# A four-way gated scan whose output is summed by accumulating transposes, with the layer norm on turned tiles and a new order of the parts

## The chip, the core and the metric

The kernel runs on one core of one Trainium2 chip. A core has a tensor engine (PE, with a separate row PEld for its weight loads), a vector engine (DVE), a scalar engine (ACT), a general engine (POOL, GpSimd) and a queue that issues transfers (SP). Each engine takes its instructions in the order of the program and waits for the others by semaphores. The metric is the time of one execution on the device in microseconds; the median of three runs before the change is 16998.98 us (16979.7 to 17001.8).

## The reference

The model has two layers. The second, a bidirectional selective scan, is the same in both kernels and matters here only because it starts after the first is done. The first layer, cut to what it computes, for x of shape (8, 192, 64, 64):

```python
x = conv1x1(x, W_in)                       # 192 -> 384 channels
x = depthwise_conv3x3(x, W_dw) + b_dw
x_proxy = conv1x1(x, W_xd)                 # 384 -> 16 channels
ws, Ls, Us, Ds = (conv1x1(x_proxy, w) for w in (W_w, W_l, W_u, W_d))
xs = [x, x.T, x reversed, x.T reversed]    # 4 directions over the last axis
Gl, Gm, Gr = normalize_w(ws)               # each / (|Gl| + |Gm| + |Gr| + 1e-7)
# scan in chunks of 8 columns; step over the column in the chunk, all chunks at once
h = 0
for each column j of a chunk:
    h = L * x + Gl * h_up + Gm * h + Gr * h_down    # neighbours along the rows
out = h * Us + xs * Ds
y = sum over the 4 directions of w_m[d] * out[d]
y = layernorm2d(y)                         # over the 384 channels
y = grn(y)                                 # scaled by each channel's norm over the image
return conv1x1(y, W_out)                   # 384 -> 192 channels
```

All of it is float32.

## The kernel before

The 384 channels are three blocks of 128 partitions. An image has 64 x 64 positions, handled as rows of 512 elements.

Each of the 8 images passes through two stages. The first, of 24 *units* (three channel blocks by eight strips of 8 rows), makes the convolved input `xc`. A unit's `begin` (from L137) multiplies by `W_in` on PE (L143), writes the centre tap from ACT (L147) and the two side taps by ACT (L159) and POOL (L162); its `unit` (L188) adds the six other taps on DVE (L196). The last units are followed by `proxy` (L173), which makes the 16-channel proxy `xp`, four times over on four groups of 32 partitions, so that gate products of different groups stand in different rows of the PE array.

The second stage is the *scan*: 3 channel blocks x 8 columns j x 4 directions d = 96 steps per image. A `Step` consists of small parts: `gates` (L240: four products of 16 rows by 512 columns, for the decay lambda and the three gates), `decay` (L252, ACT copies lambda out of PSUM), `entry` (L256, POOL, lambda times input), `magnitude` (L245, ACT, absolute values), `norm` (L275, two DVE additions), `log` and `exp` (L280, L285, ACT: a first reciprocal), `newton` (L290, two DVE operations that refine it), `neighbour` 0, 1, 2 (L259, DVE: gate times shifted state), `pair` (L265, POOL), `total` (L269, PE: two products with the identity add up the neighbours in the bank q), `mix` (L297, DVE), `state` (L301, POOL), `up` (L305, PE: the products for D, `pd`, and U, `pu`), `direct` (L308, ACT copies pd to dx), `bypass` (L312, POOL: dx times input, and at the fourth direction the third's dx is added to it, the joined bypass), `output` (L317, DVE: hu = pu times state), `add` (L321, PE: products with the identity that accumulate hu and dx of four directions in the bank yp) and `store` (L337, ACT copies yp to y once in four steps). Steps with j = 0 have no previous state, and do without the gates, the norm, the total and the mix.

PSUM has eight banks: one each tagged gl, gm, q and yp, and two each tagged gr and c. Lambda's product, pd and pu take turns on the two banks of c.

`scan` (L347) writes out the order by hand. One round of its loop (L361 to L385) works on four steps at once: the newest (`s0`), the two before, the oldest (`s3`, whose adds are made) and the next, whose gates are made. `tc.manual_schedule()` keeps each engine's instructions in the order in which the program gives them. On PE a round is total of s1, gates of the next, add hu of s3, add dx of s3, then D and U of s1. On DVE it is neighbours 2 and 0 of s0, Newton of s1, neighbour 1, the two additions of norm, hu of s2 and the mix of s1. So hu of s2 stands ahead of the mix of s1.

`Norm` (L388) does the layer norm of the image before, in ten parts beside the first units of the next image; units are left out after two of the parts. Channels are on partitions, so the mean over channels and the mean of squares are products with a constant matrix on PE (L399, L413), with three DVE subtractions (L404), three ACT squares (L408), a log, an exponent (L419, L420) and three DVE operations for the root (L421 to L423), three POOL products (L442) and three ACT squares with a sum (L430) for each j. `project_out` (L460) follows: the channel scaling, folded into the output weights, and 16 output products (L499), copies (L503) and transfers to `mid`, spread over the later units by the list `PARTS`.

Of the kernel before, what the change touches and what calls it, by code (L numbers as in the profile page):

```python
# [15 lines left out]
P = 128  # L16
CM = 192
KM = 96
# [15 lines left out]
JOINED = 2  # L34
UNITS = NC * CHUNK

PARTS = [0] * 8 + [1, 1, 1, 2, 1, 1, 1, 1, 1, 1, 1, 1, 1, 1, 1, 1]
# [4 lines left out]
ROWS = {GL: (0, 0), GM: (1, 0), GR: (2, 0), GLAM: (3, 0), GU: (0, 1), GD: (1, 1)}  # L42


@with_exitstack
def kernel(ctx: ExitStack, tc: tile.TileContext, x, w_in, dw, vecs, w_xd, w_gate, w_m, w_out, mid):
# [9 lines left out]
    big = ctx.enter_context(tc.tile_pool(name="l0_big", bufs=6))  # L56
# [46 lines left out]

    states = []
# [8 lines left out]
    class Image:  # L113
# [6 lines left out]
        def __init__(self, b):  # L120
            self.b = b
            self.x = x[b].rearrange("(k p) h w -> p k (h w)", p=KM)
            self.xc, self.xins, self.banks = [], {}, {}
            self.xp = p1.tile([P, CHUNK, CHUNK, HW], F32, tag="xp", name=f"xp_{b}")
            self.u = 0
            for u in range(4):
                self.load(u)
            for u in range(2):
                self.begin(u)
# [7 lines left out]
        def begin(self, u):  # L137
            c, r = divmod(u, CHUNK)
            if r == 0:
                self.xc.append(big.tile([P, HW, HW], F32, tag="big", name=f"xc_{self.b}_{c}"))  # L140
# [5 lines left out]
            self.load(u + 4)  # L146
# [26 lines left out]
        def proxy(self, r):  # L173
            pp = bank("c", f"pp_{self.b}_{r}")
            for c in range(NC):
                nc.tensor.matmul(
                    pp,
                    w_xd_sb[:, c, :],
                    self.xc[c][:, 8 * r : 8 * r + 8, :].rearrange("p h w -> p (h w)"),
                    start=(c == 0),  # L180
                    stop=(c == NC - 1),
                )
            nc.scalar.copy(
                self.xp[:, :, :, 8 * r : 8 * r + 8].rearrange("p j n h -> p h n j"),
                pp.rearrange("p (h n j) -> p h n j", n=CHUNK, j=CHUNK),
            )

        def unit(self):  # L188

            u, self.u = self.u, self.u + 1  # L190
            if u + 2 < UNITS:
                self.begin(u + 2)
            c = u // CHUNK
            for t in (0, 1, 2, 6, 7, 8):
                acc, part = self.shifted(u, t)
                nc.vector.scalar_tensor_tensor(  # L196
                    acc, part(self.banks[u]), dw_sb[:, c, t : t + 1], acc, ALU.mult, ALU.add
                )
            if u >= UNITS - CHUNK + 2:
                self.proxy(u % CHUNK - 2)  # L200
# [17 lines left out]
    class Step:  # L218
# [4 lines left out]
        def __init__(self, tag, xc, xp, wg, d, j):  # L223
            self.tag, self.xc, self.xp, self.wg, self.d, self.j = tag, xc, xp, wg, d, j
# [7 lines left out]
        def gate(self, kind, tag):  # L232
# [4 lines left out]
            nc.tensor.matmul(dst, self.wg[r, at, self.d, :], flat(self.xp[r, self.j]), start=True, stop=True)  # L237
# [37 lines left out]
        def norm(self):  # L275
            if self.j:
                for i in range(2):
                    nc.vector.tensor_add(self.g[2], self.g[2], flat(self.ab[i]))  # L278
# [11 lines left out]
        def newton(self):  # L290

            if self.j:
                s, rc = self.g[2], flat(self.rc)
                nc.vector.scalar_tensor_tensor(s, s, 1e-7, rc, ALU.add, ALU.mult)
                nc.vector.scalar_tensor_tensor(rc, s, 2.0, rc, ALU.subtract, ALU.mult)
# [16 lines left out]
        def bypass(self):  # L312
            nc.gpsimd.tensor_mul(self.dx, self.dx, direction(self.xc, self.d, self.j))  # L313
            if self.d == JOINED + 1:
                nc.gpsimd.tensor_add(self.dx, self.dx, self.before.dx)
# [5 lines left out]
        def add(self, i):  # L321


            if self.d == 0 and i == 0:
                self.yp = bank("yp", f"yp_{self.tag}")
            elif i == 0:
                self.yp = self.before.yp
            if i == 0 or self.d != JOINED:
                nc.tensor.matmul(
                    self.yp,  # L330
                    ident,
                    flat((self.hu, self.dx)[i]),
                    start=(self.d == 0 and i == 0),
                    stop=(self.d == ND - 1 and i == 1),
# [6 lines left out]
    class Nothing:  # L341


        def __getattr__(self, part):
            return lambda *args: None

    def scan(b, xc, xp):  # L347


        ys, steps = [], [Nothing()] * 4  # L350
        for c in range(NC):
            wg = w_gate_sb[:, :, :, c * P : (c + 1) * P]
            ys.append(big.tile([P, CHUNK, CHUNK * HW], F32, tag="big", name=f"y_{b}_{c}"))
            for j in range(CHUNK):
                steps += [Step(f"{b}_{c}_{j}_{d}", xc[c], xp, wg, d, j) for d in range(ND)]
                for step in steps[-ND:]:
                    step.y = ys[c][:, j, :]
        for before, step in zip(steps[4:], steps[5:]):
            step.before = before
        steps += [Nothing()] * 4  # L360
        for s3, s2, s1, s0, ahead in zip(steps, steps[1:], steps[2:], steps[3:], steps[4:]):  # L361
            s2.state()
            s0.neighbour(2)
            s0.neighbour(0)
            s0.entry()
            s1.newton()
            s1.total()
            s0.neighbour(1)
            s0.pair()
            s0.magnitude(2)  # L370
            s2.direct()
            ahead.gates()
            s0.norm()
            s0.log()
            ahead.decay()
            s2.bypass()
            s3.add(0)
            s2.output()
            s3.add(1)
            ahead.magnitude(0)  # L380
            s1.up()
            s0.exp()
            s1.mix()
            ahead.magnitude(1)
            s3.store()  # L385
        return ys

    class Norm:  # L388


        def __init__(self, b, ys):
            self.b, self.ys = b, ys
            self.ss = p1.tile([P, NC, CHUNK], F32, tag="ss", name=f"ss_{b}")
            self.pm, self.squares, self.var, self.rstd = {}, {}, {}, {}

        def mean(self, j):
            self.pm[j] = bank("gr", f"pm_{self.b}_{j}")
            for c in range(NC):
                nc.tensor.matmul(self.pm[j], mean_w, self.ys[c][:, j, :], start=(c == 0), stop=(c == NC - 1))  # L399

        def center(self, j):
            for c in range(NC):
                y = self.ys[c][:, j, :]
                nc.vector.tensor_sub(y, y, self.pm[j])  # L404
                sq = self.squares[j, c] = p2.tile(
                    [P, T], F32, tag=("ab0", "ab1", "dx")[c], name=f"sq_{self.b}_{j}_{c}"
                )
                nc.scalar.activation(sq, y, AF.Square)  # L408

        def variance(self, j):  # L410
            self.var[j] = bank("c", f"pv_{self.b}_{j}")
            for c in range(NC):
                nc.tensor.matmul(self.var[j], mean_w, self.squares[j, c], start=(c == 0), stop=(c == NC - 1))  # L413

        def root(self, j):

            r = self.rstd[j] = p2.tile([P, T], F32, tag="rc", bufs=3, name=f"rstd_{self.b}_{j}")
            v = self.var[j]
            nc.scalar.activation(r, v, AF.Ln, bias=eps5)  # L419
            nc.scalar.activation(r, r, AF.Exp, scale=-0.5)  # L420
            nc.vector.scalar_tensor_tensor(v, v, 1e-5, r, ALU.add, ALU.mult)  # L421
            nc.vector.tensor_mul(v, v, r)
            nc.vector.scalar_tensor_tensor(r, v, 3.0, r, ALU.subtract, ALU.mult)  # L423

        def response(self, j):

            for c in range(NC):
                y = self.ys[c][:, j, :]
                sq = p2.tile([P, T], F32, tag="hu", name=f"sq2_{self.b}_{j}_{c}")
                nc.scalar.activation(  # L430
                    sq,
                    y,
# [6 lines left out]
        def scale(self, j):  # L439
            for c in range(NC):  # L440
                y = self.ys[c][:, j, :]
                nc.gpsimd.tensor_mul(y, y, self.rstd[j])  # L442

        def parts(self):

            for j in range(CHUNK + 2):
                if j < CHUNK:
                    self.mean(j)
                if 0 <= j - 1 < CHUNK:
                    self.root(j - 1)  # L450
                    self.scale(j - 1)
                if j > 1:
                    self.response(j - 2)
                if j < CHUNK:
                    self.center(j)
                yield
                if j < CHUNK:
                    self.variance(j)

    def project_out(b, ys, ss):  # L460

        gr = p1.tile([P, NC + 1], F32, tag="gr", name=f"gr_{b}")
        gx, rg = gr[:, :NC], gr[:, NC:]
        nc.vector.tensor_reduce(gx, ss, AX.X, ALU.add)
        nc.scalar.activation(gx, gx, AF.Sqrt)
        nc.scalar.preload_act_table_set(ACT_SET)
        yield
        pg = bank("c", f"pg_{b}", (P, 1))
        for c in range(NC):
            nc.tensor.matmul(pg, mean_w, gx[:, c : c + 1], start=(c == 0), stop=(c == NC - 1))  # L470
        nc.vector.tensor_scalar_add(rg, pg, 1e-6)
        nc.vector.reciprocal(rg, rg)
# [615 lines left out]
```

## Time and profile before

| what | value |
| --- | --- |
| median of 3 runs | 16998.98 us (16979.7 to 17001.8) |
| the profiled execution | 16973.27 us |
| its span on the core | 16971.4 us |
| mean granted clock of TensorE | 0.903 of full |
| busy share of the span: PE, DVE, ACT, POOL | 84%, 90%, 72%, 89% |
| first layer, until its last projection is done | about 5973 us of the span |
| scan steps in the first layer | 768, of which 672 with j > 0 |

The page gives each engine's busy time and, in forty equal slices, its busy share in tenths; the row PEclk is the clock that TensorE was granted, in tenths of full speed. In groups and timeline rows, "q<-q,ident 128x512 f32 x4" is the output, the inputs, the shape and the number of instructions; a float32 product of 512 columns is two instructions. Matmuls overlap, so the start of the next block, and not a block's own length, tells what a block costs. The bracket behind a row of waits names the instruction that ended an idle time.

### The profile page before, as it was taken

Reading aid. Unit: us, or ns where it says so; the run is one execution under the profiler, and the core shown is the slowest. Engines: PE = TensorE matmul, PEld = TensorE weight load, DVE = VectorE, ACT = ScalarE, POOL = GpSimd, SP = SyncE. Lnnn points to the kernel's source line nnn. Section 1 sums busy time; section 2 is a strip of 40 time slices with the busy share of each in tenths; the row PEclk is TensorE's granted clock in tenths of the full one; section 3 lists DMA queues with packets and bytes.
Section 4 is the critical chain, followed back from the end, with each engine's and each line's share of the span. In section 5 each row is a group of like instructions: output and inputs, shape, how many; then the busy total and the mean of one; then the engine's idle time right before and its main releaser. Section 6 shows DMA issues by size and latency. Waiting matters only on the chain.

```text
span 16971.4 us, 183983 instructions
## 1 busy us (share of the span) xinstructions
PE 14236.2 (84%) x58320; PEld 7740.8 (46%) x58320; DVE 15279.7 (90%) x14474; ACT 12149.0 (72%) x25963; POOL 15186.0 (89%) x9955
## 2 busy tenths in 40 slices
PE   9999999999999977777777777777777777777777
PEld 2333333333333345555555555555555555555555
DVE  8888888888887779999999999999999999999999
ACT  5656666666666667777777777777777777777777
POOL 7787978778787779999999999999999999999999
PEclk8999999999999988888888888888888888888888
DMA  1001010010100022222222222222222222222222
GB/s 30 24 7 30 1 30 8 23 30 1 30 1 26 2 96 105 105 105 105 104 106 104 106 104 106 104 106 104 106 104 106 104 106 104 106 104 106 104 103 87
DMA packets 695519, 1249.43 MB, mean 74 GB/s; under 512 B 311768, under 2 KB 378672, under 8 KB 694544
## 3 DMA queue, kind: packets, MB, share of 16 engines
q1 hardware_dynamic: 694144, 1237.37, 19.9%
q8 instruction: 461, 7.55, 0.2%
q14 instruction: 514, 4.21, 0.1%
q10 hardware_dynamic: 400, 0.29, 0.0%
HBM read 1178.77 MB, written 58.72 MB: 73 GB/s over the span
## 4 chain that ended last, share of the span: by engine, by line
POOL 23%; DVE 15%; DMA 9%; ACT 8%; issue 6%; PE 4%; SPq 0%; DVEq 0%; POOLq 0%; ACTq 0%
POOL hs L861 15%; DVE da L875 11%; DMA c_sb<-bc 8%; ACT da L867 3%; POOL hs L882 3%; DVE hs L882 3%; POOL lg L768 1%; POOL e L766 1%; POOL dt L770 1%; PE pz L712 1%; POOL dtx L773 1%; DMA b_sb<-bc 1%; PE pc L700 1%; PE dbl_ps L731 1%; PE yp L887 1%
## 5 line engine op out<-in xcount | busy, mean ns | idle before, releaser
L861 POOL TENSOR_TENSOR hs<-dtx,b_sb 128x1022 f32<-128x1022 f32 x3072 | 7157.5, 2357 | 61.3 <-DMA b_sb<-bc 35.2
L875 DVE TENSOR_TENSOR_SCAN da<-da,hs 128x1024 f32<-128x1024 f32 x2560 | 5852.3, 2286 | 421.6 <-ACT hs L870 391.2
L867 ACT ACTIVATE da<-dt,a 128x512 f32<-128x512 f32 x6144 | 4247.9, 691 | 182.6
L887 PEld LDWEIGHTS yp<-ident,hs 128*128 128x128 f32 x24576 | 3022.9, 150 | 1000.1 <-issue 743.0
L887 PE MATMUL yp<-ident,hs 128*128 128x128 f32 x24576 | 3353.4, 287 | 67.1 <-DVE hs L882 59.8
L882 DVE TENSOR_TENSOR hs<-da,c_sb 128x1024 f32<-128x1024 f32 x2560 | 3129.2, 1222 | 88.7
L237 PE MATMUL g<-xp,w_gate_sb 16*128 16x512 f32 x8640 | 1812.6, 657 | 60.5 <-ACT dx L310 51.6
L700 PE MATMUL pc<-xr,conv_diag 128*128 128x512 f32 x3072 | 1542.8, 627 | 182.8 <-ACT dt L756 162.5
L878 ACT COPY state<-da 128x2 f32<-128x2 f32 x2560 | 400.8, 157 | 1626.0 <-DVE hs L882 1617.1
L820 PE MATMUL po<-out_w,z 128*128 128x192 f32 x3072 | 828.3, 420 | 748.2 <-ACT xc L704 365.3
L263 DVE TENSOR_TENSOR q<-g,h 128x512 f32<-128x512 f32 x2016 | 1353.7, 685 | 113.2 <-PE g L237 68.6
L273 PE MATMUL q<-q,ident 128*128 128x512 f32 x2688 | 1333.1, 618 | 0.0
L875 DVE TENSOR_TENSOR_SCAN hs<-da,hs 128x1024 f32<-128x1024 f32 x512 | 1168.8, 2283 | 143.1 <-ACT hs L870 87.4
L283 ACT ACTIVATE rc<-g,eps 128x512 f32<-128x512 f32 x672 | 462.2, 688 | 1119.2 <-DVE g L278 1119.2
L678 PE MATMUL pi<-xT,in_w 96*128 96x512 f32 x1536 | 955.2, 760 | 317.3 <-ACT z L812 312.2
L313 POOL TENSOR_TENSOR dx<-dx,xc 128x512 f32<-128x512 f32 x768 | 1079.7, 1406 | 155.2 <-ACT dx L310 132.7
L882 POOL TENSOR_TENSOR hs<-hs,c_sb 128x1024 f32<-128x1024 f32 x512 | 1206.7, 2357 | 1.8 <-ACT state L878 1.6
L712 PE MATMUL pz<-in_w,xT 96*128 96x384 f32 x2048 | 849.6, 541 | 421.3 <-ACT y L843 231.9
L237 PEld LDWEIGHTS g<-xp,w_gate_sb 16*128 16x128 f32 x8640 | 493.5, 188 | 1304.9 <-DVE q L263 395.9
L820 PEld LDWEIGHTS po<-out_w,z 128*128 128x128 f32 x3072 | 653.0, 245 | 829.6 <-ACT xc L704 395.3
L267 POOL TENSOR_TENSOR q<-q,q 128x512 f32<-128x512 f32 x672 | 853.6, 1270 | 193.7 <-DVE q L263 188.1
L257 POOL TENSOR_TENSOR lam<-lam,xc 128x512 f32<-128x512 f32 x672 | 942.1, 1402 | 32.1 <-ACT lam L254 32.1
(145 smaller groups left out, 25264.4 us busy)
## 6 DMA issues: line engine op xcount, KB each, us to landing
b_sb<-bc SPq DMA_DIRECT2D x1024, 512.0 KB, 9.1
c_sb<-bc SPq DMA_DIRECT2D x1024, 512.0 KB, 8.9
xin<-in_x_dram SPq DMA_DIRECT2D x192, 384.0 KB, 3.6
mid<-ot SPq DMA_DIRECT2D x128, 192.0 KB, 2.1
xt<-mid SPq DMA_DIRECT2D x64, 384.0 KB, 10.0
out_dram<-y SPq DMA_DIRECT2D x64, 384.0 KB, 2.6
bc<-dbl SPq DMA_DIRECT2D x128, 64.0 KB, 1.6
b<-bc SPq DMA_DIRECT2D x128, 8.0 KB, 7.3
```

The source lines that it names most:

```text
L237: nc.tensor.matmul(dst, self.wg[r, at, self.d, :], flat(self.xp[r, self.j]), start=True, stop=True)
L263: nc.vector.tensor_mul(self.q[i], rows(self.g[i]), self.h[:, :, i : i + HW])
L273: nc.tensor.matmul(self.sum, ident, flat(term), start=(i == 0), stop=(i == 1))
L313: nc.gpsimd.tensor_mul(self.dx, self.dx, direction(self.xc, self.d, self.j))
L700: nc.tensor.matmul(pc, self.m.conv_w[:, c, t, :], self.xr[c][:, t : t + T], start=(t == 0), stop=(t == 3))
L712: nc.tensor.matmul(pi, self.tokens.xT[:, i, s * P : (s + 1) * P], self.m.in_w[:, i, CI:], start=(i == 0), stop=(i == 1),)
L820: nc.tensor.matmul(self.po[:, s, :], self.z[:, 2 * half + s, c * P : (c + 1) * P], self.m.out_w[:, c, :], start=(c == 0), stop=(c == NC - ...
L861: nc.gpsimd.tensor_mul(self.hs[:, :, 1:], dtx, self.p.b_sb[self.g][:, :, 1:])
L867: nc.scalar.activation(self.da[:, n, :], self.p.dt[self.c], AF.Exp, scale=self.p.m.a[:, self.c, at : at + 1])
L875: nc.vector.tensor_tensor_scan(h, da, hs, 0.0, ALU.mult, ALU.add)
L882: engine.tensor_mul(self.hs, self.h, self.p.c_sb[self.g])
L887: nc.tensor.matmul(self.p.yp[self.c][:, s, :], self.hs[:, n, s * P : (s + 1) * P], ident, is_transpose=True, start=False, stop=(self.g == ...
```

## The change

It touches the first layer alone.

- `add` no longer multiplies by the identity. It turns each 128 x 128 piece of hu or dx by a transpose that accumulates in yp: four transposes for hu and four for dx. The result in yp, and in y, has positions on partitions and channels along the row.
- The joined bypass goes: dx of every direction is added by itself on PE.
- `Norm` works on the turned y. For each j and each of 4 slices DVE takes mean and variance over 384 channels (`stats`: bn_stats, bn_aggr); for each pair of j, ACT makes a log and an exponent and POOL seven small operations (`root`); POOL scales each slice (`scale`). `back` turns it back by 12 transposes for each j; ACT copies the result to `y_of` and takes the squares for the sum.
- `xc` and `y` are single constant tiles (`xc_all`, `y_all`) in place of six rotating slots.
- The order is no longer a written loop. Each part of each unit, step and norm has a slot, a number relative to its unit or step, and all parts are issued in order of their slots (`UNIT_PLAN`, `PROXY_PLAN`, `NORM_PLAN`, `STEP_PLAN`). `norm` and `newton` are split in two, the six taps in two halves.

In the built kernel a round for the newest step k then reads: PE: total(k-1), add hu(k-3), gates(k+1), add dx(k-3), pd(k-1), pu(k-1). DVE: neighbour 0 (k), Newton's first (k-1), neighbour 1 (k), Newton's second (k-1), the additions of norm (k), mix(k-1), neighbour 2 (k+1), hu(k-2). ACT: magnitude 2 (k), lambda(k+1), magnitude 0 (k+1), log(k), magnitude 1 (k+1), exp(k), dx(k-1). POOL: state(k-2), entry(k), pair(k), bypass(k-2). On the banks c, pd(k-1) follows lambda(k+1), and pu(k-1) follows the bank that hu(k-2) reads.

```diff
+STEP_PLAN = {
+    "neighbour 0": 0.04,
+    "entry": 0.04,
+    "neighbour 1": 0.12,
+    "newton 0": 1.12,
+    "total": 1.14,
+    "newton 1": 1.16,
+    "pair": 0.16,
+    "magnitude 2": 0.18,
+    "add 0": 3.19,
+    "norm 0": 0.2,
+    "gates": -0.76,
+    "add 1": 3.3,
+    "decay": -0.6,
+    "magnitude 0": -0.6,
+    "norm 1": 0.41,
+    "log": 0.43,
+    "mix": 1.46,
+    "magnitude 1": -0.5,
+    "neighbour 2": -0.49,
+    "up": 1.53,
+    "output": 2.69,
+    "exp": 0.77,
+    "bypass": 2.84,
+    "direct": 1.86,
+    "store": 3.96,
+    "state": 1.98,
+}
...
         def bypass(self):
             nc.gpsimd.tensor_mul(self.dx, self.dx, direction(self.xc, self.d, self.j))
-            if self.d == JOINED + 1:
-                nc.gpsimd.tensor_add(self.dx, self.dx, self.before.dx)
...
             if self.d == 0 and i == 0:
-                self.yp = bank("yp", f"yp_{self.tag}")
+                self.yp = bank("yp", f"yp_{self.tag}", (P, BLOCKS, P))
             elif i == 0:
                 self.yp = self.before.yp
-            if i == 0 or self.d != JOINED:
+            term = flat((self.hu, self.dx)[i])
+            for s in range(BLOCKS):
                 nc.tensor.matmul(
-                    self.yp,
+                    self.yp[:, s, :],
+                    term[:, s * P : (s + 1) * P],
                     ident,
-                    flat((self.hu, self.dx)[i]),
-                    start=(self.d == 0 and i == 0),
-                    stop=(self.d == ND - 1 and i == 1),
+                    is_transpose=True,
+                    start=(self.d == 0 and i == 0 and s == 0),
+                    stop=(self.d == ND - 1 and i == 1 and s == BLOCKS - 1),
                 )
...
+        def stats(self, j):
+            pair = j // 2
+            if j % 2 == 0:
+                self.mv[pair] = p2.tile([P, 2 * BLOCKS, 2], F32, tag="mv", name=f"mv_{self.b}_{pair}")
+                self.rstd[pair] = p2.tile([P, 2 * BLOCKS], F32, tag="rstd", name=f"rstd_{self.b}_{pair}")
+            for s in range(BLOCKS):
+                st = p2.tile([P, 6], F32, tag="st", name=f"st_{self.b}_{j}_{s}")
+                nc.vector.bn_stats(st, yT[:, j, s, :])
+                nc.vector.bn_aggr(self.mv[pair][:, j % 2 * BLOCKS + s, :], st)
+
+        def root(self, pair):
+
+            m, v, r = self.mv[pair][:, :, 0], self.mv[pair][:, :, 1], self.rstd[pair]
             nc.scalar.activation(r, v, AF.Ln, bias=eps5)
             nc.scalar.activation(r, r, AF.Exp, scale=-0.5)
-            nc.vector.scalar_tensor_tensor(v, v, 1e-5, r, ALU.add, ALU.mult)
-            nc.vector.tensor_mul(v, v, r)
-            nc.vector.scalar_tensor_tensor(r, v, 3.0, r, ALU.subtract, ALU.mult)
...
+            nc.gpsimd.tensor_scalar_add(v, v, 1e-5)
+            nc.gpsimd.tensor_mul(v, v, r)
+            nc.gpsimd.tensor_mul(v, v, r)
+            nc.gpsimd.tensor_scalar_add(v, v, -3.0)
+            nc.gpsimd.tensor_mul(r, v, r)
+            nc.gpsimd.tensor_mul(m, m, r)
+            nc.gpsimd.tensor_scalar_mul(m, m, -1.0)
+
+        def scale(self, j):
+            for s in range(BLOCKS):
+                y, at = yT[:, j, s, :], j % 2 * BLOCKS + s
+                nc.gpsimd.tensor_scalar(
+                    y, y, self.rstd[j // 2][:, at : at + 1], self.mv[j // 2][:, at, 0:1], ALU.mult, ALU.add
+                )
+
+        def back(self, j):
...
+            banks = []
             for c in range(NC):
+                pt = bank(("gr", "gr", "c")[c], f"pt_{self.b}_{j}_{c}")
+                for s in range(BLOCKS):
+                    nc.tensor.transpose(pt[:, s * P : (s + 1) * P], yT[:, j, s, c * P : (c + 1) * P], ident)
+                banks.append(pt)
+            for c in range(NC):
+                nc.scalar.copy(y_of[c][:, j, :], banks[c])
+                sq = p2.tile([P, T], F32, tag="hu", name=f"sq_{self.b}_{j}_{c}")
                 nc.scalar.activation(
                     sq,
-                    y,
+                    banks[c],
                     AF.Square,
                     bias=ln_b[:, c : c + 1],
                     scale=ln_w2[:, c : c + 1],
                     accum_out=self.ss[:, c, j : j + 1],
                 )
...
+            for k, step in enumerate(steps):
+                for part, slot in STEP_PLAN.items():
+                    part, *args = part.split()
+                    at(base + UNITS + 4 + k + slot, getattr(step, part), *map(int, args))
...
     with tc.manual_schedule():
+        for _, _, part, args in sorted(plan, key=lambda entry: entry[:2]):
+            part(*args)
```

## The prediction

> **What bounds the kernel now.** I read the page first: the clock row and the busy rows by slices.
>
> ```profile
> span 16971.4 us, 183983 instructions
> PE   9999999999999977777777777777777777777777
> DVE  8888888888887779999999999999999999999999
> PEclk8999999999999988888888888888888888888888
> ```
>
> The first layer is slices 1 to 14 (its last projection ends near 5973 us). The diff leaves the second layer alone, and the chain that ended last runs through it, so whatever the first layer gains or loses moves the end one to one. TensorE is 90% busy or more in those slices, VectorE 80 to 90%.
>
> Next the windows view over four groups of four scan steps (columns: window, sum, then busy time with count of PE, weight load, DVE, ACT, POOL, then granted clock):
>
> ```profile
> 5344.00:5436.00 92.00, 92.00 (x314) 29.94 (x312) 90.31 (x146) 61.65 (x116) 88.48 (x69) 1.00 0.00 1
> ```
>
> PE never idles, at full clock. The y copies L339 on ACT mark a group: 4605.05 to 4628.02 us is 22.97, or 5.743 a step. The timeline shows the step:
>
> ```profile
> 5382.59 1.99 PE L273 MATMUL q<-q,ident 128*128 128x512 f32 x4
> 5384.27 1.42 DVE L278 TENSOR_TENSOR g<-g,ab 128x512 f32<-128x512 f32 x2
> 5384.51 1.14 PE L237 MATMUL g<-xp,w_gate_sb 16*128 16x512 f32 x8
> 5385.58 1.13 PE L329 MATMUL yp<-hu,ident 128*128 128x512 f32 x2
> 5385.61 0.68 DVE L319 TENSOR_TENSOR hu<-g,h 128x512 f32<-128x512 f32 x1
> 5386.20 0.68 DVE L299 TENSOR_TENSOR rc<-q,rc 128x512 f32<-128x512 f32 x1
> 5386.54 1.02 PE L329 MATMUL yp<-dx,ident 128*128 128x512 f32 x2
> 5387.49 1.13 PE L237 MATMUL g<-xp,w_gate_sb 16*128 16x512 f32 x4
> 5388.55 1.98 PE L273 MATMUL q<-q,ident 128*128 128x512 f32 x4
> ```
>
> Start to start: total 1.92, four gates 1.07, add hu 0.96, add dx 0.95, down and up gate 1.06: 5.96, or 5.01 in the step without a dx add; (3 x 5.96 + 5.01)/4 = 5.72, the measured step. Note that hu (L319) comes before the mix (L299), during the adds: the up gate, which needs hu's bank, finds it free.
>
> Last, the clock, from windows of 3.41 us, the first pair of rows from the scan's light j = 0 steps, the second from layer two:
>
> ```profile
> 5655.85:5659.27 3.42, 2.75 (x8) 0.59 (x6) 0.69 (x1) 0.59 (x1) 2.07 (x2) 1.00 0.00 0
> 5659.27:5662.68 3.41, 3.41 (x7) 1.00 (x6) 0.00 (x0) 0.59 (x1) 3.01 (x3) 0.50 0.00 0
> ```
>
> ```profile
> 7488.81:7492.22 3.41, 2.19 (x21) 1.95 (x18) 3.41 (x3) 3.25 (x7) 3.41 (x3) 1.00 0.21 2
> 7492.22:7495.63 3.41, 0.67 (x6) 0.68 (x7) 3.41 (x3) 3.03 (x8) 3.20 (x3) 1.00 0.70 257
> 7495.63:7499.05 3.42, 3.42 (x11) 2.03 (x10) 3.39 (x3) 2.59 (x7) 3.31 (x2) 0.50 1.02 416
> ```
>
> The clock halves in the window after a weak one. Weak does not mean idle: the first row has PE busy 2.75 of 3.42, yet the next is at 0.50, since most of it is 16-row gates. Weighing streaming time by rows/128, that row has 0.51 of adds plus 0.31 of gates, 0.24 of the window. Done so over all windows of the trace that stand at 1.00, one below about 0.37 is followed by 0.50 and one above 0.42 is not, with some 25 exceptions in 4,000; a half window with over 0.7 is followed by 1.00. The scan's steps have (1.72 + 0.75 x 0.86 + 0.86 + 0.48 + 0.21)/5.743 = 0.68, evenly spread.
>
> **The change, part by part.** *A. Adds.* Eight 128x128 transposes replace hu's and dx's 512-column adds. Layer two has them:
>
> ```profile
> 7488.65 1.04 PE L887 MATMUL yp<-ident,hs 128*128 128x128 f32 x8
> 7489.53 0.60 PE L657 MATMUL pt<-ident,xt 128*96 128x128 f32 x4
> ```
>
> Eight in 0.88 is 0.11 each, so the eight cost 0.88 and PE's work per step falls from 5.72 to about 4.9. The joined POOL add L315 (1.27 us every fourth step) goes as well; POOL falls to 5.2. VectorE keeps nine operations, about 5.58 start to start, which would be the new floor.
>
> *A. Order.* The built kernel's queues say otherwise. In slot k PE issues total(k-1), add hu(k-3), gates(k+1), add dx(k-3), then down and up gate of k-1. VectorE ends the slot with mix(k-1), neighbour 2 of k+1, hu(k-2). The up gate takes the bank that hu(k-2) reads and waits for it; hu stands behind neighbour 2, which waits for the gates just issued; and PE goes by its order, so total(k), add and the next gates queue behind the up gate. That is a closed loop of one slot: hu 0.68, to PE 0.07, up gate 1.05, total 1.82, four transposes 0.44, switch 0.09, gates to their end 1.14, to VectorE 0.15, neighbour 2 0.60 = 6.04 us (handovers from the rows of before; 0.07 and 0.15 are its usual DVE to PE and PE to DVE gaps).
>
> A second loop takes two slots: gates, then ACT in its new order lam, ab0, log, ab1, exp (0.47 + 0.49 + 0.58 + 0.49 + 0.64 = 2.67), two handovers of 0.04, then Newton to hu's start on VectorE (seven operations in order, 4.35), then hu, up gate, total, add and gates as above (5.29): 12.39, or 6.19 a step. ACT's log(k) now stands behind lam and ab0 of k+1, which wait for gates. VectorE then idles some 0.6 us ahead of Newton. I take 6.19, the slower loop: 24.77 a group. Bounds: 5.58 (loops hand over faster than I read) and 6.3.
>
> *A. Clock.* In this slot PE streams total and add hu together (2.16 us, weight one), then for 4.0 us only gates (0.48 weighted), add dx (0.44) and down and up (0.21). A window of 3.41 that falls into that stretch holds 0.96 to 1.2, or 0.28 to 0.35, under the 0.37 above. Window starts from 2.05 to 3.35 us after total's start do so: about a fifth of the phases. So about every 4.4 full windows a half one follows; it holds the next total and add, weighs over 0.8, and the clock returns. One half window loses 1.3 us (PE fills three quarters of the loop) to 1.7 (all of it); I take 1.5: 6.19 x 18.4/(18.4 - 1.5) = 6.74 a step, 26.96 a group. Bounds: no loss, 24.77; one window in three, about 29.
>
> [...]
>
> There are 8 images x 21 groups = 168 with j > 0: 168 x (26.96 - 22.97) = **+670**.
>
> *B. Groups with j = 0.* Within a scan there are two per image, 16 in all. First to last y copy of an image is 519.8 to 527.4 us; less 21 x 22.97 that is 18.7 to 22.5 each, partly at half clock. They have gates, lam and dx only; PE loses 3.2 us of adds and POOL 1.27, the half clock stays. I take -4 each, **-65**; bounds -8 and +2.
>
> *C. Seven stages between images* (last y copy to the next first: 207.7 to 213.9 us). In 5130 to 5330 PE is busy 181.63 of 200 at clock 0.91, DVE 152.31, so PE leads, DVE follows. Out go 48 mean and variance matmuls (L399, L413) of 0.86 = 41 us of PE, 24 subtractions and 24 root operations of VectorE (1.87 + 2.07 per j = 31 us), 24 squares and 16 logs and exps of ACT (25 us), 24 POOL products (L442, 1.274: 31 us). In come 96 transposes (10.5 us), 32 pairs of bn_stats and bn_aggr on 384 columns (layer two's pair on 192 takes 0.47; between that and twice it, 15 to 30 us, I take 0.67 = 21), 24 PSUM copies (0.6: 14 us) plus 8 short logs and exps on ACT, 32 POOL tensor_scalar on 384 columns, which no row shows: 0.75 x 1.27 = 0.95 by columns, bounds 0.5 and 1.9, and 28 small POOL operations of 0.2. POOL stays near 36 us against 31. But the stage also waits for the first units' ACT and POOL parts (7 to 8 us a unit in the first part of the stage) that do not change, and the new interleaving puts the squares behind the copies on ACT (4.8 us per j). I take the 10 us that VectorE sheds and 3 for PE: -13 each, **-91**; bounds -40 and +20 (POOL scaling at 1.9).
>
> *D. End of the last image.* Nothing else runs beside the norm, 7.7 to 9 us per part in ten parts; mean, variance and root fall out of the chain, back copies come in. **-25**, bounds -45 and 0.
>
> Other edits (one big xc and y tile instead of pool slots, loads and proxies at planned slots) cost nothing: the same DMAs are issued some four units ahead, and xin lands in 3.6 us; without that cover a unit would wait those 3.6.
>
> **Sum** against the profiled execution of 16973.27: + 670 - 65 - 91 - 25 = 17,462. The median of the runs is 26 higher, so **17,490**.
>
> **Rivals.** *The clock holds* (the gates weigh more than rows/128, or the slot's phases miss the weak stretch): 168 x (24.77 - 22.97) = +302, less 181: 17,094, with the 26 17,120. For it: the margin is 0.02 to 0.09 of a window. Against: the first clock row above, where gates alone did not hold it.
>
> *Faster: the loops close sooner.* The gain of B, C and D is 181 us, so with the clock held the change wins if a step stays under 5.743 + 181/672 = 6.01 us, 0.03 below loop one. At VectorE's floor of 5.58 it is 672 x -0.163 - 181 = -291, 16,710; at 5.85, -109, 16,890. For it: matmul ends are modelled, and handovers of 0.1 decide. Against: both loops must be overstated, and the clock must hold.
>
> *Nothing moves*: a step of 5.96 to 6.06 at full clock.
>
> **How the numbers follow.** Clock lost 0.58, giving 17,300 to 17,750 (its own range); clock held and slower 0.18; within 0.2% (about 34 us, what a measurement of this kernel can tell) 0.07; faster 0.17. The range takes 17,750 at the top, leaving about 0.07 above (29 a group would give 17,830), and goes down to 16,890, leaving 0.1 below.
>
> **What would show it.** Right: groups of 24.8 to 27.5 us; PE idle before the up gate and total, released by hu; VectorE idle before Newton, released by ACT's exp; scan windows with a mean clock near 0.9; a unit stage a little shorter; L315 gone. Wrong: groups under 24 us at clock 1.00 with VectorE filled, or a unit stage that waits for POOL's scaling.

## The result and the profile after

The changed kernel takes 18583.6 us (median of 4 runs, 18563.6 to 18583.94), against 16989.34 for the kernel before (four runs): 1.0936 times as long, 95% interval 1.0917 to 1.0955. The forecast, slower, was right; 17,490 and a range that ended at 17,750 were far too low. The profiled execution took 18563.6 us, its span is 18561.7.

The lines of the page that answer to those of before:

```profile
span 18561.7 us, 191394 instructions
PE   9999999999999999777777777777777777777777
DVE  6666666666666666699999999999999999999999
PEclk7676767676777676888888888888888888888888
```

TensorE still looks full, VectorE has fallen from 8 to 6 tenths, and the clock row, 8 and 9 before, alternates between 7 and 6 for the whole first layer. All of the loss lies there: the second layer takes 10,998 us after the last projection, 11,000 before. By the y copies on ACT the first layer splits like this:

| part | before | after | difference | forecast |
| --- | --- | --- | --- | --- |
| 8 scans, first to last y copy | 524.9 us each | 740.2 | +1722 | +670 - 65 |
| 7 stages between | 210.8 | 195.2 | -109 | -91 |
| last y copy to the last projection | 124.6 | 95.8 | -29 | -25 |
| start to the first y copy | 172.1 | 179.2 | +7 | none |

The stages came out near the forecast. The scan is at half clock for 64% of its time. Where the clock stays at half, the timeline shows a step that repeats exactly (all of PE's rows, and the one of hu):

```profile
7381.61 3.78 PE L335 MATMUL q<-q,ident 128*128 128x512 f32 x4
7385.19 1.06 PE L389 MATMUL yp<-ident,hu 128*128 128x128 f32 x4
7386.18 2.09 PE L299 MATMUL g<-xp,w_gate_sb 16*128 16x512 f32 x8
7388.20 1.11 PE L389 MATMUL yp<-ident,dx 128*128 128x128 f32 x4
7389.02 0.68 DVE L378 TENSOR_TENSOR hu<-g,h 128x512 f32<-128x512 f32 x1
7389.24 2.65 PE L299 MATMUL g<-xp,w_gate_sb 16*128 16x512 f32 x4
7391.82 3.78 PE L335 MATMUL q<-q,ident 128*128 128x512 f32 x4
```

Total to total is 10.21 us. The closed loop can be read: hu starts at 7389.02 and is done at 7389.70, the up gate (second half of the block that begins at 7389.24) ends in time for total at 7391.82, and behind total queue the add and the next gates. The trace's clock windows are 3.413 us long (16 of them are the 54.61 us of the last row below), so three of them are 10.24 us. The windows view around this step (behind the five engines stands the clock, before the two DMA columns):

```profile
7346.69:7350.10 3.41, 3.41 (x4) 0.89 (x4) 2.89 (x6) 2.14 (x5) 2.54 (x4) 0.50 0.01 2
7350.10:7353.51 3.41, 3.41 (x11) 1.74 (x13) 1.23 (x2) 0.00 (x0) 1.84 (x3) 0.50 0.00 0
7353.51:7356.93 3.42, 3.29 (x17) 1.05 (x9) 1.89 (x3) 2.57 (x6) 2.18 (x2) 1.00 0.00 0
7356.93:7360.34 3.41, 3.41 (x5) 1.34 (x5) 3.19 (x5) 1.05 (x3) 1.85 (x2) 0.50 0.00 0
7360.34:7363.75 3.41, 3.29 (x20) 1.51 (x19) 2.23 (x4) 1.61 (x4) 3.12 (x3) 1.00 0.00 0
7363.75:7367.17 3.42, 3.42 (x15) 1.49 (x18) 2.68 (x5) 2.02 (x5) 1.22 (x2) 1.00 0.00 0
7367.17:7370.58 3.41, 3.28 (x16) 1.17 (x16) 3.25 (x6) 2.34 (x5) 3.40 (x4) 1.00 0.00 0
7370.58:7425.19 54.61, 54.61 (x126) 22.63 (x125) 32.24 (x50) 20.96 (x40) 29.49 (x23) 0.50 0.00 0
```

Weighed by rows/128 as in the prediction, the first seven rows hold about 0.54, 0.85, 0.29, 0.94, 0.44, 0.67 and 0.28: of the full windows, those with 0.29 and 0.28 are followed by half and those with 0.44 and 0.67 by full; of the half ones, the one with 0.54 is followed by half, those with 0.85 and 0.94 by full. Then the last row, sixteen half windows on end: they hold 0.73, 0.72, 0.41, then 0.75, 0.72, 0.41, then 0.76, 0.71, 0.41, and so on, the same three again and again since the step and three windows differ by 0.03 us, until one has crept up to 0.78. PE is "busy" all through; the busy share says nothing here. VectorE's waits do. The two largest, from 5985 to 6700 us, which holds 56 steps with j > 0 of the last image but one (groups view):

```profile
L325 DVE TENSOR_TENSOR q<-g,h 128x512 f32<-128x512 f32 x169 | 115.4, 684 | 106.6 <-PE g L299 106.6
L360 DVE TENSOR_TENSOR rc<-q,rc 128x512 f32<-128x512 f32 x56 | 38.6, 690 | 52.6 <-PE q L335 52.6
```

The neighbours wait for the gates, 1.9 us a step, and the mix for the total, 0.9 us; both are PE's, in a scan that is mostly at half speed. Before, in 16 steps at full clock, the same two groups hardly waited:

```profile
L263 DVE TENSOR_TENSOR q<-g,h 128x512 f32<-128x512 f32 x49 | 32.9, 684 | 0.6 <-ACT ab L250 0.5
L299 DVE TENSOR_TENSOR rc<-q,rc 128x512 f32<-128x512 f32 x16 | 10.9, 681 | 0.0
```

### The profile page after: what moved, and what is told of

It reads as the page before. It is cut to its first block, busy times and chain, and to the rows that moved or that the text cites. A ratio compares the mean times of both kernels' runs of the same rounds, so it can differ in the third digit from the quotient of the medians.

```text
span 18561.7 us, 191394 instructions
## 1 busy us (share of the span) xinstructions
PE 15756.1 (85%) x61776; PEld 8787.9 (47%) x61776; DVE 15261.8 (82%) x14602; ACT 12006.5 (65%) x25899; POOL 14964.1 (81%) x10051
## 4 chain that ended last, share of the span: by engine, by line
POOL 19%; DVE 16%; ACT 8%; DMA 7%; issue 6%; PE 4%; SPq 0%; DVEq 0%; POOLq 0%; ACTq 0%
POOL hs L877 12%; DVE da L891 11%; DMA c_sb<-bc 6%; ACT da L883 3%; DVE hs L898 3%; POOL hs L898 2%; POOL lg L784 1%; POOL e L782 1%; PE pz L728 1%; POOL dt L786 1%; DMA b_sb<-bc 1%; DVE hs L891 1%; POOL dtx L789 1%; PE pc L716 1%; PE yp L903 1%
## 5 line engine op out<-in xcount | busy, mean ns | idle before, releaser
L299 PE MATMUL g<-xp,w_gate_sb 16*128 16x512 f32 x8640 | 2959.9, 847 | 62.6 <-ACT lam L316 2.4
L316 ACT COPY lam<-g 128x512 f32<-128x512 f32 x768 | 450.0, 586 | 3164.4 <-PE g L299 3160.9
L335 PE MATMUL q<-q,ident 128*128 128x512 f32 x2688 | 2166.4, 952 | 0.0
L319 POOL TENSOR_TENSOR lam<-lam,xc_all 128x512 f32<-128x512 f32 x672 | 941.2, 1401 | 547.4 <-ACT lam L316 533.0
L335 PEld LDWEIGHTS q<-q,ident 128*128 128x128 f32 x2688 | 693.0, 285 | 1360.7 <-issue 1355.8
L364 POOL TENSOR_TENSOR h<-lam,rc 128x512 f32<-128x512 f32 x672 | 853.5, 1270 | 544.9 <-DVE rc L360 541.9
L299 PEld LDWEIGHTS g<-xp,w_gate_sb 16*128 16x128 f32 x8640 | 862.1, 238 | 794.5 <-issue 477.1
```

The source lines that it names most:

```text
L299: nc.tensor.matmul(dst, self.wg[r, at, self.d, :], flat(self.image.xp[r, self.j]), start=True, stop=True)
L319: nc.gpsimd.tensor_mul(self.lam if self.j else self.hc, self.lam, direction(self.xc, self.d, self.j))
L335: nc.tensor.matmul(self.sum, ident, flat(term), start=(i == 0), stop=(i == 1))
```

## The experiments

Each run changes the changed kernel, unless it says otherwise. Two theories stood at the start: that the clock costs the time, because the order leaves windows with little weighed work in them, and that the order's waits alone cost it.

**Zero transposes in the weak stretch.** Y keeps its value, since what is added is zero.

```diff
+FILL = 8
...
+    zeros = const.tile([P, P], F32, name="zeros0")
+    nc.gpsimd.memset(zeros, 0.0)
...
             term = flat((self.hu, self.dx)[i])
+            for s in range(FILL if i == 1 else 0):
+                nc.tensor.matmul(
+                    self.yp[:, s % BLOCKS, :], zeros, ident, is_transpose=True, start=False, stop=False
+                )
```

> Edit: eight transposes of a zero tile accumulate into the open yp bank ahead of each dx add, so y keeps its value and PE gets 0.88 us more work per step, in the stretch where it waits. Theory (the clock is lost because windows of 3.41 us fall into a weak stretch): the weakest window rises from 0.28 to about 0.53, the clock stays near 1.00 in the scan, a group of four steps takes 24.2 to 25.2 us and the run 17,000 to 17,200 us although PE has more to do. Rival (the new order's waits cost the time and the low clock only shows that PE waits): no better than 18,580. Second rival (transposes, or transposes of zeros, do not count for the clock): clock still near 0.65 in the scan, 18,600 to 19,200 us.

Measured: 17138.19 us (1.0092 of before, 1.0071 to 1.0112). Twelve steps of the last image, windows view and the group ahead of which VectorE waits:

```profile
5700.00:5774.60 74.60, 74.60 (x384) 39.39 (x382) 66.79 (x109) 45.00 (x87) 62.72 (x49) 1.00 0.00 1
```

```profile
L359 DVE SCALAR_TENSOR_TENSOR g<-g,rc 128x512 f32<-128x512 f32 x12 | 8.4, 700 | 7.3 <-ACT rc L352 7.3
```

The clock is 1.00, the scan is at half for 4% of its time, and the median group is 24.88 us. 6144 more transposes made the kernel 1,445 us faster: the clock is shown to be most of the cost, and transposes of zeros count for it. What is left, 24.88 against 22.97, is put down to the loops, forecast at 24.77 (a run below takes the slower of them apart); VectorE idles 7.3/12 = 0.61 us a step ahead of Newton, forecast at 0.6.

**The same work as plain products.**

```diff
                     ident,
-                    is_transpose=True,
                     start=(self.d == 0 and i == 0 and s == 0),
```

> Edit: in the changed kernel's own order the four transposes of each add are plain float32 products with the identity (same result, 128 columns each), which takes twice as long on PE: about 0.22 us each for 0.11, 0.88 us more per step. Theory (clock): the add of dx in the weak stretch weighs 0.86 in place of 0.44, the weakest window about 0.40 to 0.45, the clock holds nearly everywhere, the loop is 0.43 longer, 6.5 us a step: 17,250 to 17,500 us, some 1,100 us faster than the changed kernel with more work. Rival (PE's work in the loop costs): 19,000 us or more.

Measured: 17452.91 us (1.0277, 1.0256 to 1.0297), median group 26.19 us, half clock 8% of the scan. The theory's forecast held. Each add is eight instructions on PE in place of four (96 of dx in twelve steps, 6060 to 6140), the one of hu inside the closed loop, and the run is 1,131 us faster than with transposes.

**The same zero transposes elsewhere**, behind the add of hu, where PE streams anyway (FILL is 8 again).

```diff
                     stop=(self.d == ND - 1 and i == 1 and s == BLOCKS - 1),
                 )
+            for s in range(FILL if i == 0 else 0):
+                nc.tensor.matmul(
+                    self.yp[:, s % BLOCKS, :], zeros, ident, is_transpose=True, start=False, stop=False
+                )
```

> Edit: the same eight zero transposes per step in the changed kernel, but right behind the add of hu, where PE is busy anyway, in place of the weak stretch ahead of the dx add. PE's work and its activity per step are those of the run that gave 17,138 us; the one-slot loop is 0.88 longer, 6.92 us. Theory (what counts is the weakest 3.41 us, still 0.28 to 0.35): the clock still falls, half for 25 to 60% of the scan, 17,900 to 18,900 us. Rival (the mean activity over a step counts): clock above 0.97 in the scan and 17,500 to 17,700 us.

Measured: 17754.05 us (1.0454, 1.0433 to 1.0475); median group 27.87, or 6.97 a step; half clock 7% of the scan. Neither expectation held. The clock still falls, 100 times in the eight scans where the fill of the weak stretch leaves 21, so the mean over a step is not what counts. (The full windows of this scan hold 0.56 in the mean; those of the run with the old order, next, hold 0.56 too, and it falls 26 times.) But 96 of the 100 falls last one window, and 14 to 26 full windows lie between most. A step of 6.97 is close to two windows (6.83), so the phase moves by only 0.14 a step and reaches the weak stretch seldom; and with 0.88 more next to total, a half window soon carries enough. That the drift explains the rarity, and the added weight the quick return, is argued from these numbers, not shown by a run of its own.

**The old order of the step**, transposes and the new norm kept. Only slots change (an excerpt):

```diff
-    "total": 1.14,
-    "add 0": 3.19,
-    "gates": -0.76,
-    "add 1": 3.3,
-    "mix": 1.46,
-    "neighbour 2": -0.49,
-    "up": 1.53,
-    "output": 2.69,
+    "total": 1.1,
+    "gates": -0.8,
+    "add 0": 3.3,
+    "add 1": 3.34,
+    "output": 2.32,
+    "up": 1.38,
+    "mix": 1.42,
+    "neighbour 2": 0.02,
...
```

> Edit: only the slots of the scan step are changed, to the order that the loop of the kernel before had; transposes, layer norm, unit and norm slots and the missing joined bypass stay. Theory (the order closed the loop and emptied a stretch of PE): hu is early again, total, gates and adds follow one another, the weakest window is about 0.46, the clock holds; a step takes between 5.58 us (VectorE's nine operations) and 5.74, and with the shorter stage between images the run is 16,680 to 16,880 us. Rival (the transposes take so much work from PE that the clock drops in any order): scan clock under 0.9 and over 17,300 us.

Measured: 16855.82 us (0.9925, 0.9909 to 0.9942). Four groups, windows view:

```profile
5477.30:5568.30 91.00, 91.00 (x385) 41.65 (x385) 89.91 (x146) 60.57 (x117) 84.03 (x65) 1.00 0.00 1
```

22.75 a group at full clock, VectorE busy 89.91 of 91.00: it is the bound now. So the loss belongs to the order; in steps with j > 0 the transposes alone do not lower the clock, and with the old order the change is a gain. At the light j = 0 groups the clock falls for longer than before: half clock is 14% of the scan, against 6% before, 16 stretches of 7 to 14 windows and ten single ones, where the kernel before has none above three. The gain therefore does not come from the scan, which takes 527.6 us an image for 524.9 before, but from the stages between images (195.2 for 210.8) and the end of the layer.

**One slot: hu ahead of the mix.**

```diff
-    "output": 2.69,
+    "output": 2.45,
```

> Edit: one slot, hu of step k-2 ahead of the mix and neighbour 2 instead of last on VectorE. Theory (loop and clock both count): the up gate no longer waits for the gates of the same slot, the loops fall to about 5.6 us; but total and add hu still stand together on PE, so a window can hold 0.33 and part of the half clock stays: 16,900 to 17,800 us, scan clock 0.8 to 0.97. Rival (the wait of the up gate for hu was all): clock 1.00 and 16,700 to 16,850 us. Second rival (the place of hu does not matter): 18,400 to 18,700 us.

Measured: 16972.96 us (0.9995, 0.9985 to 1.0006), the same as before. 1,611 us lie in the place of one VectorE instruction. A quarter of the groups takes 22.65 us or less, so the loops have gone; the clock is still half for 20% of the scan, in 137 stretches of which 121 are single windows; by the theory, since total and add hu still stand together:

```profile
5536.45:5727.20 190.75, 184.89 (x728) 80.71 (x727) 159.00 (x256) 110.25 (x212) 157.80 (x121) 0.88 0.00 1
```

Both parts of the theory count, and the rival that the up gate's wait was all (1.00, 16,700 to 16,850) is out.

**A longer loop.** This run tests why the half state lasts. The result of bn_stats is not used; all else is computed.

```diff
+            st = p2.tile([P, 6], F32, tag="late", name=f"late_{self.tag}")
+            nc.vector.bn_stats(st, still)
             self.hu = self.work("hu")
```

> Edit: the changed kernel with one more VectorE operation ahead of hu in each step (bn_stats of a still tile of 192 columns, 0.33 us in layer two's rows; its result is not used), which makes its closed loop longer. In the changed kernel a step at half clock takes 10.21 us, three windows are 10.24, and the half stretches last 4.05 windows on average, 59 of them 8 or more. Theory (the half state lasts because the slow step is in step with the windows, so that the same phases come back until one carries 0.77): a slow step of 10.5 us shifts by 0.27 each time, stretches of 8 or more nearly go (under 10), the mean is under 2.5, and the scan's half share falls from 0.64 to 0.35 to 0.52, so that the run is no slower or even faster although the loop is longer: 17,700 to 18,500 us. Rival (the coincidence does not matter; the half state lasts since half a clock makes windows weak): stretches as long as before, and 768 x 0.3 = 230 us more, 18,750 to 18,900 us.

Measured: 18251.47 us (1.0751, 1.0730 to 1.0773), 332 us faster than the changed kernel. VectorE's timeline shows the added operation, 0.27 us from its start to that of hu:

```profile
5300.32 0.35 DVE L380 BATCH_NORM_STATS2 late<-still 128x6 f32<-128x192 f32 x1
5300.59 0.67 DVE L382 TENSOR_TENSOR hu<-g,h 128x512 f32<-128x512 f32 x1
```

Half stretches last 1.81 windows in the mean, for 4.05; 16 are of 8 or more, for 54 (the 59 of the expectation counts those of five or more); the half share is 0.44. More long ones are left than the theory allowed, but all 16 lie at the light j = 0 groups, two an image; elsewhere none is longer than four windows. In the changed kernel 213 steps with j > 0 run at half from total to total, 210 of them in 10.21 us; here only 4 steps do, so the slow step of 10.5 us cannot be read from this trace. An operation added to the critical loop has taken 332 us off, which the rival excludes: the near equality of the slow step and three windows is what made the half stretches long. It is not the whole loss. The weak stretch is still there, and the run is 1,113 us above the one with zero transposes. And since the step at full clock is longer as well, the phases move in both states; the run does not part the two.

**Log ahead of lambda**, on top of the zero transposes of the first run (17,138 us):

```diff
-    "decay": -0.6,
-    "magnitude 0": -0.6,
+    "decay": -0.56,
+    "magnitude 0": -0.55,
```

> Edit: the changed kernel with eight zero transposes ahead of each dx add (17,138 us, group 24.88), and on ACT log of step k moved ahead of lambda and magnitude 0 of step k+1. Theory (the two-slot loop through ACT sets 6.2 us a step): VectorE's idle time of 0.6 us a step ahead of Newton goes, the one-slot loop of 6.04 is left: a group of 24.0 to 24.4 us, 16,990 to 17,070 us. Rival (the one-slot loop through the up gate sets all of it, and PE is full with the zero transposes): 24.7 to 25.0 us, 17,110 to 17,160 us.

Measured: 17029.36 us (1.0027, 1.0017 to 1.0038), median group 24.37, or 6.09 a step. The two-slot loop through ACT set the 6.22: VectorE's idle time ahead of Newton falls from 0.61 to 0.17 us a step (2.9 us in 17 steps, 5600 to 5700). That the one-slot loop, worked out at 6.04, sets what is left fits the number and is not shown by a run.

**Towards a better version**: the old order, and six zero transposes only in steps with j = 0 and j = 7.

```diff
+FILL = 6
...
+            for s in range(FILL if i == 1 and self.j in (0, CHUNK - 1) else 0):
+                nc.tensor.matmul(
+                    self.yp[:, s % BLOCKS, :], zeros, ident, is_transpose=True, start=False, stop=False
+                )
```

> Edit: the old order of the step as in the run before (16,856 us, scan at half clock for 14% of its time, in stretches of 7 to 14 windows behind the j = 0 groups), and six transposes of a zero tile ahead of the dx add of steps with j = 0 and j = 7 alone, which is where PE has little to do. Theory (what is left of the half clock is the light j = 0 groups, and it is long since a half window must carry about 0.77 to be followed by a full one): half clock in the scan under 7%, the median group stays 22.75 us (VectorE's nine operations), 16,740 to 16,810 us. Rival (those groups do not wait for PE): 16,840 to 16,900 us.

Measured: 16760.86 us (0.9868, 0.9852 to 0.9885), half clock down from 14% to 6% of the scan, median group unchanged at 22.75. Then a new order of VectorE and ACT on top of it (an excerpt; the orders of PE and POOL stay):

```diff
-    "newton 1": 1.085,
-    "output": 2.32,
-    "magnitude 0": -0.64,
-    "magnitude 1": -0.56,
-    "exp": 0.4,
+    "newton 1": 1.08,
+    "output": 2.11,
+    "magnitude 0": -0.79,
+    "magnitude 1": -0.78,
+    "exp": 0.19,
...
```

> Edit: as the run with the old order and zero transposes, but with another order of the step: VectorE neighbour 0, Newton 1, neighbour 1, Newton 2, norm 1, hu, norm 2, mix, neighbour 2 of the next, so that no operation stands right behind the one whose result it takes; ACT lambda, log and exp ahead of the next step's two magnitudes; PE as in the old order. Theory (VectorE is the bound once the clock holds, and pairs that follow each other directly cost 0.72 in place of 0.60): a group of 22.0 to 22.4 us, 16,620 to 16,740 us. Rival (hu early and norm late close another loop through log and exp, or POOL's 5.35 us and its waits lead): a group of 22.75 us or more, over 16,780 us.

Measured: 17113.07 us (1.0077, 1.0062 to 1.0092); the rival was right, 24.75 a group at a clock that is full in 94% of the scan. The groups of the last image, 5600 to 5690, show the new loop:

```profile
L328 DVE TENSOR_TENSOR q<-g,h 128x512 f32<-128x512 f32 x33 | 22.5, 684 | 11.1 <-ACT ab L315 9.1 <-PE g L302 1.9
L381 DVE TENSOR_TENSOR hu<-g,h 128x512 f32<-128x512 f32 x16 | 10.9, 681 | 14.2 <-PE g L302 14.2
```

Neighbour 0 now waits for ACT's magnitude, which I had put behind log and exp and which reads the same gate, 9.1 us in 11 steps. The larger wait, hu's for the gates, lies in the j = 0 steps: in the steps with j > 0 that the timeline shows from 5600 to 5612, hu does not wait. The last run changes the old order with zero transposes (16,761 us) by one slot alone:

```diff
-    "newton 1": 1.085,
+    "newton 1": 1.13,
```

> Edit: in the old order with zero transposes (16,761 us) one slot: Newton's second operation behind neighbour 1, so that it no longer follows the first directly. Theory (VectorE is the bound; a dependent pair costs 0.72 in place of 0.60): 0.12 a step, a group of 22.25 to 22.4 us, 16,670 to 16,720 us. Rival (the later Newton holds the bank that the next gates wait for, and PE hands it on): 22.75 us or more, 16,760 us or more.

Measured: 16675.23 us (0.9824, 0.9808 to 0.9841), median group 22.21. Its page and four groups:

```profile
span 16669.9 us, 194107 instructions
DVE  8888889889898699999999999999999999999999
```

```profile
5300.00:5388.80 88.80, 88.80 (x386) 39.35 (x385) 88.26 (x145) 60.53 (x117) 83.59 (x65) 1.00 0.00 1
```

VectorE is busy 88.26 of 88.80. The theory held: Newton's second operation starts 0.72 us behind the first in the run with 16,761 us, and here each of the two is followed 0.60 us later by the next; the group is 0.54 shorter. This is the fastest version, 1.8% under the kernel before: the parts of the change, the old order with one slot moved, and six zero transposes in steps with j = 0 and j = 7.

## Why the prediction was right and wrong

*Bound and place*: right. The whole difference lies in the first layer, and nearly all in the scan.

*The order's loops*: right. Forecast 24.77 us a group at full clock; 24.88 with the clock held by zero transposes, which add 0.88 us a step to PE. In the changed kernel itself only 12 steps run wholly at full clock, in 5.75 to 6.30 us, for 6.19. The two-slot loop was the slower, as taken, and VectorE's idle time ahead of Newton has the forecast size. One sign was wrong: PE was to show idle time ahead of the up gate; its rows show almost none, since D's product starts ahead of U's and the block of both counts as busy throughout (at full clock from 7354.99 it is 1.96 us long, for 1.13 before).

*The clock falls*: right; weak windows were followed by half, at the weight read from the trace of before. In the changed kernel's trace some 3,390 windows stand at full clock, and a threshold of 0.36 to 0.38 by rows/128 tells those followed by half with some 30 to 40 exceptions. If streaming is taken to begin 0.06 us behind the recorded start of a row, a threshold of 0.375 leaves 5 exceptions, and 2 of 4,000 in the trace of before. The weighing is my own, and it rests on the fit: with the 16-row gates counted in full the best threshold has some 345 exceptions, with transposes at half weight some 140. In the trace of before the window at 7488.81 has transposes alone, 2.0 us of them, and the next stands at 1.00; and with the zero fill the clock was 1.00 in the twelve steps above.

*How long it stays down*: wrong, and this is the step that failed. The prediction has one half window after about 4.4 full ones, because the half window "weighs over 0.8, and the clock returns", a loss of 1.5 us each and 26.96 us a group. Measured are half stretches of 4.05 windows and full ones of 2.33 in the mean. Three things were off. First, the price of the return: 0.7 was too low. By the same weighing the line that parts half windows followed by full from the others lies at 0.73 in the trace of before, at 0.74 in that of the longer loop and at 0.77 here, where only about 8% of the half windows at 0.71 to 0.74 return and 23% of those at 0.74 to 0.77; with streaming taken to begin 0.06 us late it is 0.74 to 0.76 in all three. So the line lies near 0.75 in these three traces, and the half windows of this order often hold 0.71 to 0.74. Second, the half window's phase: it need not begin with total, and may hold 0.41 to 0.76. Third, I treated the phases as random. They are not: 92 of the 272 returns fall 4.5 to 6 us after total's start, when total and the add of hu are over, and 86 of these 92 full windows are followed by half at once (96 of all 272 full stretches are one window long); and the slow step, 10.21 us, is in step with three windows. The forecast of the half windows used no length of a slow step. The loss in one half window was about right: 3.41 x (1 - 6.2/10.21) = 1.34 us, for 1.5. Their share was not: one half window in 5.4 is 19%, and the measured stretches make it 64%; the half ones alone, at 4.05 windows with 4.4 full ones between, would make it 48%, the full ones alone, at 2.33 with single half ones, 30%. With the measured shares, a mean step is 1/(0.638/10.21 + 0.362/6.2) = 8.27 us, 33.1 a group, and 168 groups cost +1,700 in place of +670.

*Groups with j = 0*: forecast -4 each; their share was not told apart under the low clock. In the old order they are where the clock falls, which the prediction let stand as "the half clock stays" without seeing that it lasts beyond them.

*Stages and tail*: -15.6 each for -13, and -29 for -25. POOL's scaling of a slice takes 0.67 us for 0.95, and bn_stats with bn_aggr 0.53 + 0.18 = 0.71 for 0.67; which engine's saving shortened the stage was not tested. The first image's +7 us was not in the sum.

*Faster rival*: its turning point, 6.01 us a step with the clock held, was sound: 6.09 a step gave 17,029, 0.3% slower than before, and 5.69 in the old order gave 0.75% faster.

## What to carry to other kernels

In the traces of before and of the changed kernel PE's clock went by the weight of the window before: full windows of 3.41 us under about 0.37 were followed by half. So look at the weakest window that a step leaves and not at the mean or the busy share; and work out the step at half clock too: here it took 10.21 us against three windows of 10.24, and half stretches lasted 4.05 windows, 1.81 with one VectorE operation more. An add by four accumulating transposes took 0.53 us to the start of the next block (changed kernel, 7360.40 to 7360.93 at full clock) where the product with the identity took 0.96, but this took weight out of the windows: keep the remaining work spread, or put the saved time back as work that changes nothing (eight zero transposes a step: -1,445 us). One VectorE instruction in another place of the order was worth 1,611 us here; before a new order is tried, follow from each bank to the operation that frees it and back.

## What I had not expected of the hardware

- More work made the kernel faster three times: eight zero transposes a step (-1,445 us), products for transposes (-1,131), and one more VectorE operation in the critical loop (-332).
- Going down and coming back lie at different weights, by the weighing above: in the traces of before and of the changed kernel full windows were followed by half under about 0.37, and half windows by full over 0.73 to 0.77. Of the windows between 0.42 and 0.70 in these two traces each was followed by one of its own state, 2,556 at full and 361 at half.
- A neighbour product on VectorE waited for ACT's read of the same PSUM gate (0.72 us in each of the two steps from 5600 to 5612 in the run with the new order), though neither writes it. The profile shows a wait for a semaphore, which the program sets; that the chip itself would delay the second read is not shown.
